# A four-layer graph network on one core: a 20-row tile in four column groups, its last ends moved into the next layer, and the last two output tiles in plain form

## The chip, the cores and the metric

The kernel runs on one core of one Trainium2 chip. The metric is the device time of one execution in microseconds (us); lower is better. A core has engines that run side by side, each in its own order: TensorE (PE, matrix products, with its weight loads listed apart as PEld), VectorE (DVE), ScalarE (ACT), GpSimd (POOL), and SyncE (SP), which here issues most DMAs. ACT and POOL issue DMAs too. Matmul results land in PSUM, which has eight banks per partition; everything else works on SBUF.

## The reference: what is computed

A graph with N = 2708 nodes, F = 256 features and a dense adjacency matrix `adj` (N x N, fp32) goes through four layers. After each layer the input is added and each row is normalised (mean 0, variance 1, eps 1e-5).

```python
# layer 0
x = layernorm(x + adj @ (x * w0))
# layer 1: graph attention, 4 heads of 64
e    = leaky_relu(src[:, :, None] + dst.T[None])      # masked by adj > 0, softmax over neighbours
x    = layernorm(x + layernorm(attn @ h) * gamma + beta)
# layer 2: three signed attention heads and two GRU cells
x    = layernorm(x + de * edge_output + dn * node_output)
# layer 3
deg  = adj.sum(1) + 1
h    = adj @ (x @ neigh_w.T) / deg
x    = layernorm(x + concat([x, h]) @ lin_w.T)
```

All arithmetic is fp32 unless noted.

## The kernel before, in words

Nodes are cut into NT = 22 tiles of 128 rows; 2708 is 21 x 128 + 20, so tile 21 has 20 rows. `adj_t` is the adjacency, padded to 22 x 128, cut into blocks of 128 x 128 that are transposed. Instructions are written in program order and a scheduler then fixes one order per engine; each engine works strictly through its own list, and semaphores tie the lists together.

**Layer 0** (L432 to L559). For each tile t a strip `adj_t[t]` (1408 KB) is loaded by SP, and `strip_matmul` (L201) adds up 22 products of 128 x 128 by 128 x 257 in one PSUM bank `acc`; the 257th column of the right side is 1 and yields the degree. An fp32 matmul shows as two PE instructions, so a tile is 44 instructions. Beside it `layer0_mask` and `layer0_own` read the strip on DVE and ACT. Then `layer0_rest(t - 1)` for the tile before: `layer0_scale` reads `acc`, `layernorm` (its `moments` use POOL for the power) and `layer1_projection`: two PE transposes (`tr`, L179), a copy by ACT, a projection (`pm`, L410), three exponentials by ACT, a product by DVE (`h`, L417), one more transpose (`pf`, L424), a copy and a DMA to `fall_d`. After the last strip, L558 and L559 run this for tiles 20 and 21, one after the other. Tile 21 uses 20 of the array's 128 columns but streams the same 257 columns per product.

**Layer 1** (L561 to L759). For each pair of column groups (`g` = 0, 2, 4: 1024, 1024 and 660 nodes) and each pair of heads `q`, a loop over the source tiles c = 0 to 21. Per c, DVE makes two weight tiles `p` (128 x 1024, L736) from a pool of six buffers, and PE multiplies them twice: `heads` (L718, results on 64 partitions, so two products side by side in the array) and `totals` (L727, results on 32 partitions, so four side by side). `step(c)`, once in each c, advances whatever generators are in the list `steps`: the ends of the group before. In g = 0 the list is empty. The last rows `h` of tiles 20 and 21 are first read at c = 20 and 21.

**Layer 2** (to L1232) ends with the generator `node`, whose pieces wait in the list `later`; `between()` runs one piece. PSUM is full there: `m1` takes one bank, `m26`, `m75`, `m43` two each, and all small work shares one bank called `bank`.

**Layer 3** (L1235 to L1283). The 2708 columns are cut in two halves of NH = 1354, the contraction in two halves as well, and each pair of chunks c (11 of them) is multiplied by a seven-product scheme (`seven`, L290) in place of eight. A half is cut in `units` of 512, 512 and 330 columns. Per unit and c, SP loads the block `p` (`load_pairs`, L240: one DMA for each run of whole tiles and contraction tile, one for each partial tile), DVE makes four sums, PE runs seven fp32 products (14 instructions) into the seven banks. At the end of a unit `gathered` (L313) combines the banks, and `rows3` (L1239) turns each tile back with two transposes, adds, normalises and stores it; its pieces run between the products of the next unit. In the first unit, `early3` chunks run beside what is left of `node`. For the third unit there is no next one: its rows run after the last product in a new set of banks (L1280 to L1283).

```python
L1279            later.append(rows3(u, y, o8))
L1280        ps_stack.close()
L1281        banks = ps_stack.enter_context(pool("ps_end", 8, space=PSUM))
L1282        while urgent or later:
L1283            between()
```

Of the kernel before, what the change touches and what calls it, by code (L numbers as in the profile page):

```python
# [19 lines left out]
P = 128  # L20
# [7 lines left out]
def kernel(  # L28
# [50 lines left out]
    MP = NT * P  # L79

    def sz(i):
        return min(P, N - i * P)
# [6 lines left out]

    def pieces(lo, w):  # L90

        while w:
            t, a = divmod(lo, P)
            b = min(P, a + w)
            yield t, a, b
            lo, w = lo + b - a, w - (b - a)

# [29 lines left out]
    x0 = [a[:, :F] for a in x0e]  # L127

    ends_at = [max(u for u, (a, w) in enumerate(units) for h in range(2) for p in pieces(h * NH + a, w) if p[0] == t) for t in range(NT)]
    by_end = sorted(range(NT), key=lambda t: ends_at[t])  # L130
# [108 lines left out]

    def load_pairs(units, u, c, s):  # L240

        a, w = units[u]
        for h in range(2):
            todo, at = list(pieces(h * NH + a, w)), 0
            while todo:

                t, lo, hi = todo.pop(0)
                n = 1
                while hi - lo == P and todo and todo[0][2] - todo[0][1] == P:
                    todo.pop(0)  # L250
                    n += 1
                m = n * (hi - lo)
                for i in range(2) if n > 1 else (slice(0, 2),):
                    src = adj_t[t : t + n, :, 2 * c + i, :].rearrange("t p n -> p t n") if n > 1 else adj_t[t, :, 2 * c : 2 * c + 2, lo:hi]
                    dst = s[:, i, h, at : at + m]
                    nc.sync.dma_start(dst.rearrange("p (t n) -> p t n", n=P) if n > 1 else dst, src)  # L256
                at += m
# [55 lines left out]
    def gathered(pool, m, w, wide, tag, bufs=1):  # L313

        m1, m26, m75, m43 = m
        m1s = pool.tile([P, wide], F32, tag="m1s", name="m1s", bufs=2)
        nc.scalar.copy(m1s[:, :w], m1[:, :w])
        y = pool.tile([P, FC, 2, wide], F32, tag=tag, name=tag, bufs=bufs)
        yq = y.rearrange("p f h w -> p (f h) w")[:, :, :w]
        nc.vector.tensor_tensor(  # L320
            yq[:, 0::3], m1s[:, None, :w].to_broadcast([P, 2, w]), m26[:, :, :w], ALU.add
        )
        nc.vector.tensor_tensor(
            yq[:, 1:3], yq[:, 3:4].to_broadcast([P, 2, w]), m75[:, :, :w], ALU.add
        )
        nc.vector.tensor_tensor(yq[:, 3], yq[:, 1], m75[:, 1, :w], ALU.add)
        return y, nc.vector.tensor_tensor(yq[:, 1:3], yq[:, 1:3], m43[:, :, :w], ALU.add)
# [57 lines left out]
    if True:  # L385
# [13 lines left out]
        if True:  # L399
# [5 lines left out]
            def layer1_projection(pool, t):  # L405
                n = sz(t)
                xt = transposed(ps_t, pool, xs[t], n, "xt")
                pm = ps_t.tile([P, 4, P], F32, tag="tr", name="pm").rearrange("p i q -> p (i q)")
                for f in range(FC):
                    nc.tensor.matmul(  # L410
                        pm[:n, : F + 2 * H], xt[:, f, :n], w1_a[:, f], start=(f == 0), stop=(f == FC - 1)
                    )
                nc.scalar.activation(rise[:n, t, :], pm[:n, F + H : F + 2 * H], AF.Exp, scale=1.0 - ALPHA)
                nc.scalar.activation(hs[t][:n, :, HD], pm[:n, F + H : F + 2 * H], AF.Exp, scale=ALPHA)
                fall = pool.tile([P, H], F32, tag="fall", name="fall", bufs=4)
                nc.scalar.activation(fall[:n], pm[:n, :H], AF.Exp, scale=ALPHA - 1.0)
                nc.vector.tensor_tensor(  # L417
                    hs[t][:n, :, :HD],
                    pm[:n, H : H + F].rearrange("p (h d) -> p h d", d=HD),
                    hs[t][:n, :, HD:].to_broadcast([n, H, HD]),  # L420
                    ALU.mult,
                )
                pf = ps_t.tile([P, 4, P], F32, tag="tr", name="pf")
                nc.tensor.transpose(pf[:H, 0, :n], fall[:n], ident[:n, :n])  # L424
                turned = pool.tile([H, P], F32, tag="turned", name="turned")
                nc.scalar.copy(turned[:, :n], pf[:H, 0, :n])
                nc.gpsimd.dma_start(fall_d[:, t * P : t * P + n], turned[:, :n])

                for g in [g for g, (lo, hi) in enumerate(spans[:4]) if hi == t + 1]:
                    load_fall(falls[g // 2], g, nc.gpsimd)  # L430

            with pool("l0", 2) as l0:  # L432
                w0_b = l0.tile([P, F], F32, name="w0_b", bufs=1)
                nc.scalar.dma_start(w0_b, bcast(w0, F))

# [26 lines left out]

                def layer0_rest(t, acc=None):
                    n = sz(t)
                    if acc is not None:
                        layer0_scale(t, acc)
                    nc.vector.tensor_tensor(xs[t][:n], xs[t][:n], x0[t][:n], ALU.add)
                    layernorm(xs[t], xs[t], n)
                    layer1_projection(l0, t)


                ahead = 3
                with pool("prep", side="right") as prep:
# [47 lines left out]
                    for t in range(ahead):  # L521
                        layer0_rest(t)
                    nw = weights(prep, "nw", neigh_w)
# [26 lines left out]
                nc.sync.dma_start(beta_b, bcast(beta, F))  # L550
                for t in range(ahead + 1, NT):
                    s = load_strip(l0, t)
                    last, acc = acc, ps_acc.tile([P, 512], F32, tag="acc", name="acc")
                    strip_matmul(acc[: sz(t), :FE], s, sz(t), lambda c: x0e[c])
                    layer0_mask(t, s)
                    layer0_own(t, s)

                    layer0_rest(t - 1, last)  # L558
                layer0_rest(NT - 1, acc)  # L559

            l1 = keep_stack.enter_context(pool("l1", 2))  # L561
            if True:

# [123 lines left out]
                for g in range(0, len(spans), 2):  # L687
# [6 lines left out]
                    cols = [(lo * P - at, width(lo, hi)) for lo, hi in segs]  # L694
                    sums, steps, halves = [], [], []

# [14 lines left out]
                    for q in range(H // 2):  # L711
# [20 lines left out]
                        for c in range(NT):  # L732
                            ps = []
                            for i in range(2):
                                p = l1.tile([P, 2 * W], F32, tag="p", name="p", bufs=6)
                                nc.vector.scalar_tensor_tensor(  # L736
# [264 lines left out]
    with (  # L1001
# [143 lines left out]

        def by_tiles(lo, w, src, ends):

            tiles, at = [], 0
            for t, c0, c1 in pieces(lo, w):
                got = src(at, c1 - c0)  # L1150
                at += c1 - c0
                if c1 - c0 < sz(t):
                    first = t not in ends
                    if first:
                        ends[t] = nleft.tile([P, FC, P], F32, tag=f"yt{t}", name=f"yt{t}")
                    nc.gpsimd.tensor_copy(ends[t][:, :, c0:c1], got)
# [78 lines left out]
        def complete(u):  # L1235

            return [t for t in by_end if ends_at[t] == u]

        def rows3(u, y, o8):  # L1239

            a, w = units[u]
            for h in range(2):
                for t, src in by_tiles(h * NH + a, w, lambda at, n: y[:, :, h, at : at + n], shared3):
                    n = sz(t)
                    o = o8[:, complete(u).index(t)]
                    pt = bank()
                    for f in range(FC):
                        nc.tensor.transpose(pt[:n, f * P : (f + 1) * P], src[:, f, :n], ident)
                    nc.vector.scalar_tensor_tensor(
                        o[:n], pt[:n, :F], rdeg[:n, t : t + 1], o[:n], ALU.mult, ALU.add  # L1250
                    )
                    mean, rs = moments(o, n)
                    nc.vector.scalar_tensor_tensor(mean, mean, -1.0, rs, ALU.mult, ALU.mult)
                    nc.scalar.activation(o[:n], o[:n], AF.Identity, scale=rs, bias=mean)
                    (nc.scalar if t % 2 else nc.sync).dma_start(out[t * P : t * P + n, :], o[:n])
                    yield


        lead = sorted(range(MH), key=lambda c: max(ends_at[2 * c], ends_at[2 * c + 1]))
        hq = {}  # L1260
        for u, (_, w) in enumerate(units):
            m = accumulators()
            for i, c in enumerate(lead):
# [6 lines left out]
                pa = nright.tile([P, 2, 2, W], F32, tag="p", name="p", bufs=3)  # L1270
                load_pairs(units, u, c, pa)
                if i == MH - 3:
# [6 lines left out]
            later.append(rows3(u, y, o8))  # L1279
        ps_stack.close()  # L1280
        banks = ps_stack.enter_context(pool("ps_end", 8, space=PSUM))  # L1281
        while urgent or later:  # L1282
            between()  # L1283
    hold_stack.close()
# [263 lines left out]
```

## Time and profile before

| what | value |
|---|---|
| median of three runs | 1902.06 us (1900.7, 1902.06, 1903.51) |
| the profiled execution, its own time | 1902.43 us |
| its span, first to last instruction | 1900.7 us |
| granted TensorE clock, mean of the span | 0.992 |
| PE busy | 1848.4 us (97%), 7475 instructions |
| DVE busy | 1283.9 us (68%) |
| ACT, POOL busy | 689.6 us (36%), 249.6 us (13%) |
| longest PE groups | L309 (seven products), L718 and L727 (layer 1), L203 (layer 0) |

In a page of the profile, a group of instructions is a line such as `L203 PE MATMUL acc<-turn,strip 128*128 128x257 f32 x836 | 191.6, 380 | 0.0`: source line, engine, operation, output and inputs by their names in the program, the weights' shape, the output's shape, the count; then busy time, mean duration of one in ns, and idle time of the engine just before. Matmuls are pipelined, so one lasts longer than the distance from its start to the next one's. That distance, the pitch, is what a stream of them costs; it is read from a timeline. In a timeline a line has start, length, engine, line, operation and count, and in brackets the idle time before it with what ended it. A table of windows gives the busy time of each engine in a stretch and, as PEclk, the share of full clock that TensorE was granted.

### The profile page before, as it was taken

Reading aid. Unit: us, or ns where it says so; the run is one execution under the profiler, and the core shown is the slowest. Engines: PE = TensorE matmul, PEld = TensorE weight load, DVE = VectorE, ACT = ScalarE, POOL = GpSimd, SP = SyncE. Lnnn points to the kernel's source line nnn. Section 1 sums busy time; section 2 is a strip of 40 time slices with the busy share of each in tenths; the row PEclk is TensorE's granted clock in tenths of the full one; section 3 lists DMA queues with packets and bytes.
Section 4 is the critical chain, followed back from the end, with each engine's and each line's share of the span. In section 5 each row is a group of like instructions: output and inputs, shape, how many; then the busy total and the mean of one; then the engine's idle time right before and its main releaser. Section 6 shows DMA issues by size and latency. Waiting matters only on the chain.

```text
span 1900.7 us, 22827 instructions
## 1 busy us (share of the span) xinstructions
PE 1848.4 (97%) x7475; PEld 1024.5 (54%) x7479; DVE 1283.9 (68%) x2279; ACT 689.6 (36%) x1418; POOL 249.6 (13%) x415
## 2 busy tenths in 40 slices
PE   8999989999999999999899999999999999999996
PEld 6888832223345887887344444444445555654444
DVE  4344469999797666554557888686877758855655
ACT  4444410033143204111455665555565555311101
POOL 1211210001012411000001001110200101211201
PEclk9999989999999999999999999999999999999998
DMA  8334400010002657554756666453554444733653
GB/s 293 130 145 152 167 23 1 1 29 7 17 1 55 150 130 208 129 126 111 209 141 187 184 166 177 115 159 97 165 150 119 121 113 129 191 111 98 194 155 107
DMA packets 432922, 235.89 MB, mean 124 GB/s; under 512 B 172150, under 2 KB 420620, under 8 KB 430364
## 3 DMA queue, kind: packets, MB, share of 16 engines
q1 hardware_dynamic: 416158, 207.40, 39.4%
q0 software_dynamic: 7760, 21.20, 3.4%
q10 hardware_dynamic: 8878, 5.76, 1.0%
q8 instruction: 61, 1.00, 0.2%
q14 instruction: 65, 0.53, 0.1%
HBM read 221.61 MB, written 12.65 MB: 123 GB/s over the span
## 4 chain that ended last, share of the span: by engine, by line
PE 85%; DVE 4%; DMA 4%; issue 2%; ACT 2%; POOL 1%; SPq 1%; ACTq 0%; DVEq 0%; POOLq 0%
PE m L309 39%; PE acc L718 11%; PE acc L203 8%; PE bank L1083 7%; PE den L727 6%; PE gate L958 4%; PE bank L1059 3%; PE bank L1134 2%; PE acc L510 1%; POOL bn_rs L167 1%; DMA strip<-in_adj_t_dram 1%; PE pm L410 1%; DVE p L1217 1%; SPq L256 1%; DMA blk<-in_adj_t_dram 1%
## 5 line engine op out<-in xcount | busy, mean ns | idle before, releaser
L736 DVE SCALAR_TENSOR_TENSOR p<-fall_b,rise,mask 128x1024 f32<-128x1024 f32 (+1 forms) x264 | 293.1, 1155 | 34.7 <-PE den L727 17.8
L1213 ACT ACTIVATE p<-st,e_neg 128x1024 f32<-128x1024 f32 (+1 forms) x198 | 197.2, 1040 | 206.6 <-PE m L309 202.6
L309 PE MATMUL m<-s,xq 128*128 128x512 f32 (+3 forms) x660 | 230.1, 467 | 0.0
L718 PE MATMUL acc<-p,h 128*64 128x512 f32 (+2 forms) x1056 | 216.6, 553 | 0.2 <-ACT sum L749 0.2
L203 PE MATMUL acc<-turn,strip 128*128 128x257 f32 (+1 forms) x836 | 191.6, 380 | 0.0
L309 PE MATMUL m<-p,xq 128*128 128x512 f32 (+1 forms) x396 | 183.1, 544 | 0.6 <-DVE p L297 0.3
L1216 ACT ACTIVATE p<-p 128x1024 f32<-128x1024 f32 (+1 forms) x198 | 178.9, 943 | 0.2
L309 PE MATMUL m<-p,x 128*128 128x512 f32 (+1 forms) x396 | 169.7, 547 | 5.1 <-DVE p L1217 4.8
L1217 DVE TENSOR_TENSOR p<-p,blk 128x1024 f32<-128x1024 f32 (+1 forms) x132 | 143.3, 1104 | 42.1 <-ACT p L1216 22.1
L203 PEld LDWEIGHTS acc<-turn,strip 128*128 128x128 f32 (+1 forms) x836 | 151.5, 185 | 25.3 <-issue 0.5
L309 PEld LDWEIGHTS m<-s,xq 128*128 128x128 f32 x660 | 124.3, 190 | 74.7 <-issue 58.2
L296 DVE TENSOR_TENSOR s<-p 128x512 f32<-128x512 f32 (+1 forms) x132 | 83.4, 633 | 119.6 <-PE m L309 104.3
L718 PEld LDWEIGHTS acc<-p,h 128*64 128x64 f32 x1056 | 70.5, 137 | 140.9 <-issue 131.7
L309 PE MATMUL m<-s,x 128*128 128x512 f32 (+3 forms) x330 | 127.4, 468 | 0.0
L727 PE MATMUL den<-p,h 128*32 128x512 f32 (+2 forms) x1056 | 118.2, 551 | 2.6 <-DVE p L736 2.6
L309 PEld LDWEIGHTS m<-p,x 128*128 128x128 f32 x396 | 74.8, 191 | 79.3 <-issue 60.9
L309 PEld LDWEIGHTS m<-p,xq 128*128 128x128 f32 x396 | 74.5, 190 | 78.1 <-issue 60.9
L452 ACT ACTIVATE below<-strip 128x384 bf16<-128x384 f32 x132 | 78.5, 594 | 70.9 <-DMA strip<-in_adj_t_dram 67.5
L1217 DVE TENSOR_TENSOR p<-p,turn 128x1024 f32<-128x1024 f32 (+1 forms) x66 | 72.0, 1112 | 20.3 <-ACT p L1216 12.2
L299 DVE TENSOR_TENSOR s<-p,s 128x512 f32<-128x512 f32 (+1 forms) x132 | 83.0, 629 | 2.0
L297 DVE TENSOR_TENSOR p<-p 128x512 f32<-128x512 f32 (+1 forms) x132 | 83.0, 629 | 1.7
L309 PEld LDWEIGHTS m<-s,x 128*128 128x128 f32 x330 | 61.7, 190 | 38.4 <-issue 34.1
(258 smaller groups left out, 2505.7 us busy)
## 6 DMA issues: line engine op xcount, KB each, us to landing
strip<-in_adj_t_dram SPq DMA_DIRECT2D x19, 1408.0 KB, 6.0
blk<-in_adj_t_dram SPq DMA_DIRECT2D x88, 256.0 KB, 3.3
blk<-in_adj_t_dram SPq DMA_DIRECT2D x88, 192.0 KB, 4.0
pa<-in_adj_t_dram SPq DMA_DIRECT2D x110, 128.0 KB, 2.6
turn<-in_adj_t_dram SPq DMA_DIRECT2D x44, 256.0 KB, 3.1
blk<-in_adj_t_dram SPq DMA_DIRECT2D x88, 128.0 KB, 2.4
p<-in_adj_t_dram SPq DMA_DIRECT2D x44, 256.0 KB, 3.4
turn<-in_adj_t_dram SPq DMA_DIRECT2D x44, 192.0 KB, 3.1
```

What stands on the lines that cost most here:

```text
L203: nc.tensor.matmul(acc, s[:, c, :n], rhs(c), start=(c == 0), stop=(c == NT - 1))
L296: nc.vector.tensor_tensor(s1, a21, a22, ALU.add)
L297: nc.vector.tensor_tensor(a21, a21, a11, ALU.subtract)
L299: nc.vector.tensor_tensor(s4, a12, s2, ALU.subtract)
L309: nc.tensor.matmul(dst[:, :w], lt, rt, start=start and not (one_bank and i), stop=stop and not (one_bank and i in (1, 2, 5)))
L718: nc.tensor.matmul(acc[s][i * HD : (i + 1) * HD, :ws], hs[c][:, 2 * q + i, :HD], ps[i][:, p0 : p0 + ws], **flags,)
L727: nc.tensor.matmul(den[j : j + CT, :ws], hs[c][:, 2 * q + i, HD + 1 - CT :], ps[i][:, p0 : p0 + ws], **flags,)
L736: nc.vector.scalar_tensor_tensor(p[:, :w], falls[g // 2][:, 2 * q + i, :w], rise[:, c, 2 * q + i : 2 * q + i + 1], mask[:, c, at : at + w] ...
L1083: nc.tensor.matmul(g[:, :w], lt, rt, start=(q == 0), stop=(q == len(terms) - 1))
L1213: nc.scalar.activation(p[:, :, :w], st_k[:, :, :w], AF.Relu, scale=-1.0, bias=e_neg[:, at, k : k + 1])
L1216: nc.scalar.activation(p[:, :, :w], p[:, :, :w], AF.Exp, scale=-1.0)
L1217: nc.vector.tensor_tensor(p[:, :, :w], p[:, :, :w], blk[:, i, :, :w], ALU.mult)
```

## The change

1. Layer 0's tile 21 (20 rows, at most CT = 32) is multiplied with 32-column weights; product c writes to partitions 32 (c mod 4) and up of `acc`, so that four of them are independent groups. ACT copies `acc` to `parts`, and one product with `quarter` (a 128 x 32 sum of identity columns) adds the four groups up (`layer0_last`).
2. `layer0_rest` and `layer1_projection` become generators. Those of tiles 20 and 21, with `layer0_last` between them, are put in `steps` of layer 1's g = 0, one piece for each c. `w0_b` and `quarter` move to a pool that lives on, and the helper tiles of these two ends to layer 1's pool. The scale of tile 20 stays in layer 0.
3. Layer 1's `p` has five buffers in place of six; `m1s` in `gathered` one in place of two.
4. Layer 3 leaves the last two full tiles (19 and 20) out of the seven-product scheme. The other 2452 columns make halves of NH3 = 1226, in units of 430, 430 and 366. `pieces` walks a list of tiles, and partial tiles fall at other places.
5. After the third unit, tiles 19 and 20 are multiplied in plain form (22 products of 128 x 128 by 128 x 256 each, the strip in two loads), into `m1` and `m26`; the rows of the third unit run between them, their transposes going round `bank`, `m75`, `m43`. There is no new set of banks.
6. `row3` holds back the last steps of a row (scale, ACT, store) until the next row's moments are issued (`flush`).

The diff, cut to its core:

```diff
+    last3 = [t for t in range(NT) if min(P, N - t * P) == P][-2:]
+    tiles3 = [t for t in range(NT) if t not in last3]
+    NH3 = (N - P * len(last3)) // 2
+    n3 = -(-NH3 // W)
+    w3 = min(W, (NH3 + P // 2) // n3)
+    units3 = [(a, min(w3, NH3 - a)) for a in range(0, NH3, w3)]
...
-        m1s = pool.tile([P, wide], F32, tag="m1s", name="m1s", bufs=2)
+        m1s = pool.tile([P, wide], F32, tag="m1s", name="m1s", bufs=1)
...
+            quarter = keep.tile([P, CT], F32, name="quarter")
+            nc.vector.tensor_reduce(quarter, ident.rearrange("p (j i) -> p i j", i=CT), AX.X, ALU.add)
...
+                def layer0_rest(pool, t):
                     n = sz(t)
                     nc.vector.tensor_tensor(xs[t][:n], xs[t][:n], x0[t][:n], ALU.add)
+                    mean, rs = moments(xs[t], n)
+                    yield
+                    nc.vector.tensor_scalar(xs[t][:n], xs[t][:n], mean, rs, ALU.subtract, ALU.mult)
+                    yield
+                    yield from layer1_projection(pool, t)
...
+                def layer0_last(t, parts):
+                    pq = ps_t.tile([P, 4, P], F32, tag="tr", name="pq").rearrange("p i q -> p (i q)")
+                    nc.tensor.matmul(pq[: sz(t), :FE], quarter[:, : sz(t)], parts[:, :FE], start=True, stop=True)
+                    layer0_scale(t, pq)
+                    yield
...
+                    for c in range(NT):
+                        j = c % TILES * CT
+                        nc.tensor.matmul(
+                            acc[j : j + CT, :FE], s[:, c, :CT], x0e[c], start=(c < TILES), stop=(c >= NT - TILES)
+                        )
...
+                layer0_scale(t - 1, last)
+                layer0_mask(t, s)
+                layer0_own(t, s)
+                    parts = keepr.tile([P, W], F32, tag="sum00", name="parts0")
+                    nc.scalar.copy(parts[:, :FE], acc[:, :FE])
...
+            rest = [layer0_rest(l1, NT - 2), layer0_rest(l1, NT - 1)]
+            if sz(NT - 1) <= CT:
+                rest.insert(1, layer0_last(NT - 1, parts))
...
-                    sums, steps, halves = [], [], []
+                    sums, steps, halves = [], [itertools.chain(*rest)] if g == 0 else [], []
...
-                                p = l1.tile([P, 2 * W], F32, tag="p", name="p", bufs=6)
+                                p = l1.tile([P, 2 * W], F32, tag="p", name="p", bufs=5)
...
+        ended = []
+        def flush():
+            while ended:
+                t, o, mean, rs = ended.pop()
+                n = sz(t)
+                nc.vector.scalar_tensor_tensor(mean, mean, -1.0, rs, ALU.mult, ALU.mult)
+                nc.scalar.activation(o[:n], o[:n], AF.Identity, scale=rs, bias=mean)
+                (nc.scalar if t % 2 else nc.sync).dma_start(out[t * P : t * P + n, :], o[:n])
+        def row3(t, o, acc):
+            n = sz(t)
+            nc.vector.scalar_tensor_tensor(o[:n], acc[:n, :F], rdeg[:n, t : t + 1], o[:n], ALU.mult, ALU.add)
+            mean, rs = moments(o, n)
+            flush()
+            ended.append((t, o, mean, rs))
...
-        for u, (_, w) in enumerate(units):
+        for u, (_, w) in enumerate(units3):
...
-                load_pairs(units, u, c, pa)
+                load_pairs(units3, u, c, pa, NH3, tiles3)
...
-        ps_stack.close()
-        banks = ps_stack.enter_context(pool("ps_end", 8, space=PSUM))
-        while urgent or later:
-            between()
+        free = itertools.cycle([None, "m75", "m43"])
+        per = -(-NT // 2)
+        for t, tag in zip(last3, ("m1", "m26")):
+            o = nleft.tile([P, F], F32, tag="y", name="y", bufs=3)
+            nc.gpsimd.dma_start(o, y3_d[t])
+            acc = ps_a.tile([P, W] if tag == "m1" else [P, 2, W], F32, tag=tag, name=tag)
+            acc = acc if tag == "m1" else acc[:, 0]
+            for lo in range(0, NT, per):
+                hi = min(lo + per, NT)
+                s = nright.tile([P, 2, 2, W], F32, tag="p", name="p", bufs=3).rearrange("p i h w -> p (i h w)")
+                s = s[:, : (hi - lo) * P].rearrange("p (c n) -> p c n", n=P)
+                nc.sync.dma_start(s, adj_t[t, :, lo:hi])
+                for c in range(lo, hi):
+                    nc.tensor.matmul(acc[:, :F], s[:, c - lo], h3[c], start=(c == 0), stop=(c == NT - 1))
+                    if c % 3 == 2 and (t != last3[0] or lo):
+                        between()
+            if t == last3[-1]:
+                while urgent or later:
+                    between()
+                flush()
+            row3(t, o, acc)
+        flush()
```

## The prediction

> **What bounds the kernel now.** I read the page's busy shares first, then a table of windows by stage, then the timeline of PE at the two places where PE is not full.
>
> ```profile
> PE 1848.4 (97%) x7475; PEld 1024.5 (54%) x7479; DVE 1283.9 (68%) x2279; ACT 689.6 (36%) x1418; POOL 249.6 (13%) x415
> ```
>
> PE is busy 97% of the span, so only two things can bring much: fewer columns through PE, or the few stretches where PE stands still. The windows name two such stretches, the passage from layer 0 to layer 1 and the end:
>
> ```profile
> 242.00:262.00 20.00, 15.43 (x67) 6.71 (x65) 8.07 (x20) 2.50 (x15) 4.92 (x8) 0.91 0.20 54
> 1882.00:1901.00 19.00, 2.63 (x17) 1.63 (x15) 10.01 (x39) 4.09 (x7) 4.27 (x9) 0.71 0.15 47
> ```
>
> Of the last 19.00 us PE works 2.63. The passage, PE alone (columns: start, length, engine, line, operation, count, idle time before):
>
> ```profile
> 245.33 8.44 PE L203 MATMUL acc<-turn,strip 128*20 128x257 f32 x38
> 253.70 0.44 PE L179 MATMUL tr<-ident,x 128*128 128x128 f32 x2
> 254.60 1.16 PE L410 MATMUL pm<-w_a,xt 128*128 128x264 f32 x4 [0.46 <-ACT xt L181]
> ...
> 257.88 1.38 PE L410 MATMUL pm<-w_a,xt 128*20 128x264 f32 x4 [0.34 <-ACT xt L181]
> ...
> 262.52 1.93 PE L727 MATMUL den<-p,h 128*32 128x512 f32 x8 [2.64 <-DVE p L736]
> 264.38 5.80 PE L718 MATMUL acc<-p,h 128*64 128x512 f32 x16
> 270.11 1.93 PE L727 MATMUL den<-p,h 128*32 128x512 f32 x16
> 271.96 3.65 PE L718 MATMUL acc<-p,h 128*64 128x512 f32 x16
> ```
>
> The 20-row tile costs as much as a full one (38 instructions in 8.37 us, start to start). Then the chains of tiles 20 and 21 run end to end, and PE waits for the first weights: 262.52 - 253.70 = 8.8 us from the end of the strip to layer 1. Note also the first two source tiles of layer 1: 7.59 us (262.52 to 270.11), where the next two take 5.44 (270.11 to 275.55). The third column from the end of a windows row is the granted clock, and tells why:
>
> ```profile
> 256.00:258.00 2.00, 0.69 (x4) 0.39 (x5) 0.88 (x3) 0.54 (x4) 1.49 (x3) 1.00 0.47 126
> 258.00:260.00 2.00, 1.45 (x5) 0.28 (x3) 0.34 (x1) 0.37 (x4) 0.35 (x1) 0.62 0.36 87
> 264.00:266.00 2.00, 2.00 (x8) 0.53 (x6) 2.00 (x3) 0.00 (x0) 0.00 (x0) 0.50 0.00 0
> ```
>
> The granted clock falls at about 259 us and is half at 264 to 266. The end, last product to last store:
>
> ```profile
> 1882.01 0.72 PE L309 MATMUL m<-s,turn 128*128 128x330 f32 x2
> ...
> 1892.30 0.44 DVE L1249 SCALAR_TENSOR_TENSOR o<-bank,rdeg,o 20x256 f32<-20x256 f32 x1
> ...
> 1895.16 0.59 ACT L1254 ACTIVATE o<-o,bn_mv,bn_rs 20x256 f32<-20x256 f32 x1
> 1895.78 0.55 ACTq L1255 DMA_DIRECT2D out_dram<-o  x1
> ```
>
> Seven rows go one after the other through DVE, POOL and ACT, with no product left to hide them.
>
> **The change, part by part.** All times are of the one profiled execution (1902.43 us, of which 1900.7 are span; the 1.7 outside stay). It lies 0.4 above the median of 1902.06, inside the runs' spread of 2.8, so the sum stands for both.
>
> *Tile 21 in four groups.* In layer 1, four `totals` products side by side have a pitch, per set of four, of 0.464 us at 512 columns (16 instructions in 1.855) and of 0.354 at 384 and 276 (16 in 1.415), while one full-width instruction of 512 columns takes 0.429 (24 in 10.3 us from 1754.85). So a set costs about its widest member plus 0.03. At 257 columns a full-width one takes 8.37 / 38 = 0.220 to 0.2285 (44 in 10.05 per tile); a set then costs 0.25, and 44 instructions are 11 sets, 2.8 in place of 10. For the 34 of them that come after the last insertion (`pf` of tile 19, 245.33), 2.1 us: the strip ends at 247.5. From both sides: nothing saved if the four don't overlap (34 x 0.22 = 7.5, 5.4 us later), or 0.354 a set if some fixed cost of the four weight loads binds (0.9 later). I take 0.25, because the row at 512 columns shows four at 1.08 times one. [...]
>
> *Tile 20's end stays in the passage.* In the changed kernel's instruction order PE still has `tr`, `pm`, `pf` of tile 20 ahead of layer 1, and behind them the one product `pq` that adds up the four groups. From `tr` to the end of `pf` took 2.6 us (253.70 to 256.3); ACT now copies `parts` ahead of `xt`, 257 columns, 0.4 by the rows of L749 at 276 columns (0.39), of which 0.3 shows; `pq` is two instructions, 0.46. Layer 1 can start at 247.5 + 2.6 + 0.3 + 0.5 = 250.9. Is DVE ready? Its order has eight `p` right after `h` of tile 19, which ended at 246.05. The first `p` needs only `fall_b`; the second may wait for the strip's buffer (247.5), so two are done by 249 and the third by 250.1. Yes. 250.9 against 262.52: **-11.6**.
>
> *The clock.* 7.59 - 5.44 = 2.15 us were lost to half clock. [...] the longest gap here is 2.64 and the clock had fallen before it began, with PE at 3.43 of 6 us busy (254 to 260). [...] a half-busy stretch is enough. Judged by the trace, the changed passage (1.7 us of work in 3.4, from 247.5 to 250.9) is half-busy too, but short[...]. [...] **-2.15**; by the trace's worst, 0. I take the gain.
>
> *Tile 21's end in layer 1.* Its PE work moves into a full stretch: two `tr` (0.12), four `pm` (0.92), one `pf` (0.1), and the pieces wait for nobody's data long, being a c or more apart: **+1.25**. DVE gets ten small operations (about 3 us). It needs 2.4 of the 2.72 us per c, so it regains that in ten c, and it starts with a lead of two or three `p`; the 20 c until `h` of tile 20 is read cover ACT's and POOL's part. POOL's `fall_d` store of tile 21 is read only for g = 4, 250 us later.
>
> *Five buffers.* With PE working on two `p`, three are ahead in place of four. I followed DVE's and PE's instruction order with the trace's durations (DVE 1.20 per `p` of 1024 columns, 0.82 of 660, 0.40 per 256-column operation; PE 1.79 + 0.93 per c): no stall with five or six. With DVE 6% slower five lose 0.5. **+0.2**, between 0 and 1.
>
> *Layer 3, columns.* Pitch of an instruction: 0.4293 at 512, 0.2768 at 330, so 0.3606 at 430 and 0.3070 at 366 on a straight line. 154 instructions per unit: 154 x (2 x 0.4293 + 0.2768) = 174.9 before, 154 x (2 x 0.3606 + 0.3070) = 158.3 after, -16.6. Plain tiles: 2 x 44 x 0.2285 = +20.1. PE ends its products with all rows' transposes done but the last: 0.22 a tile, five more than at 1882, +1.1. Waits: before, those over 0.15 us add up to about 5 until 1882; one of 1.12 ahead of 1854.54, a transpose behind a DVE that stood waiting for POOL's power, goes with `flush`. Shorter products (-0.14 per pair) hide less of `node`'s bank changes; the instruction order already puts two products where one stood, so +1. Sum: PE's last product comes **+4.6** later, passage and clock aside.
>
> *Layer 3, queues.* SP issues seven loads per c now in unit 2, eight after in units 1 and 2. 32 loads took 16.37 us from 1857.84, 0.51 each, so eight take 4.1, against a c of 14 x 0.307 = 4.3 (5.05 in units 0 and 1). It fits, with little over in unit 2; three stores also stand in SP's list there, 0.4 each. The strips of the plain tiles take the buffers of chunks 9 to 11 and of the first half strip: 720 KB each, every 5.0 us, where a 1408 KB strip lands in 6.0. Costed at nothing; if late, each 1 us is 1 us. POOL's two loads of `y3_d` are issued a unit's length ahead.
>
> *Layer 3, end.* Before: 1882.57 (last product's end) to 1900.7, 18.1 us. After, one row is left: 0.35 to DVE, sum and moments 0.95, POOL 0.2 + 0.55, DVE and ACT 0.8, all from the rows of the last tile above, then 4.9 from issue to the end (1895.78 to 1900.7): 7.8. **-10.3**. The eight rows of unit 2 have eleven slots of 1.37 us, and DVE needs 1.33 for one; they begin 5 us after the unit's end, when `gathered` (2.4 us then, plus POOL's copies) is done.
>
> `m1s` and `w0_b` cost nothing: its copies are tens of us apart. Layer 2's orders are unchanged.
>
> Sum: -11.6 - 2.15 + 1.25 + 0.2 + 4.6 - 10.3 = -18.0: **1884.5 us**.
>
> **The rivals.** (1) The clock falls again. The stretch's half load speaks for it, its brevity against: +2.15, and a late `p` 1 more: 1887 to 1888. (2) Layer 3 gives nothing: strips or blocks late at the changes of unit (as at 1836.90, 0.56 us behind a load), or `node`'s waits grow by 0.14 at each of 37 bank changes (5 us), which together eat the 5.7: 1890. Against it: SP's 0.51 and the order. (3) Slower than before: small pieces. New pieces are 8, 36, 38 and 46 columns wide, 32 to 184 bytes a packet. In units 0 and 1 (1766 to 1834 us) 25846 packets took 60.2% of 16 engines, 25 ns each. Unit 1 has 2304 packets per c, 3.6 us in 5.05. Were they dearer, all 33 chunks would run at the DMAs' pace. At 34 ns it begins, at 40 the whole gain is gone, at 45 it is 1915. Against: in unit 2 now 8048 of 18291 packets are under 512 B and q1's took 53.4%, 23 ns each. (4) The four groups don't overlap: 1890.
>
> **How the numbers follow.** The sum as it stands 0.52, (1) 0.20, (2) 0.18, (4) 0.04, (3) 0.04, of which half ends slower, and 0.02 for several losses at once, half of them slower too. Low end 1881: the sum less 3.5 (waits of layer 3 gone as well). High end 1893: (1) and (2) together. A difference of 0.2% (3.8 us) is about what measurements of this kernel tell from none. Faster by more 0.94, within 0.03, slower 0.03.
>
> **What would show it.** PE's first `den` near 251 with the first two c in 5.5 us and the clock at 1.00 (right), or 0.50 in 252 to 257 (1). The 32-column products: sets of four in 0.25. Layer 1's PE never waiting for a `p` after its first. The plain products without a DMA wait, the last one some 8 us before the end. In the chunks of 366 columns PE waiting for DMA, chunk after chunk, would be (3). Wrong altogether if the passage still ends after 258, or the end is over 12 us.

## The result, and the profile after

| | before | after |
|---|---|---|
| median | 1901.38 us (4 runs, 1900.04 to 1903.51) | 1885.57 us (4 runs, 1883.11 to 1887.16) |
| profiled execution, its span | 1902.43, 1900.7 us | 1887.16, 1885.1 us |
| ratio of the times | | 0.9915, 95% interval 0.9898 to 0.9932 |

The change brings 15.8 us, where the prediction's sum was 18.0; the time of 1885.57 us lies in the predicted range of 1881 to 1893, near its 1884.5. Not every term of the sum held. PE's row of the page:

```profile
PE 1843.0 (98%) x7565; PEld 1037.4 (55%) x7565; DVE 1278.9 (68%) x2280; ACT 690.1 (37%) x1419; POOL 254.2 (13%) x419
```

PE is 5.4 us less busy in a span that is 15.6 shorter, so some 10 us were standing time. The windows of the two stretches (columns: stretch, length, PE, PEld, DVE, ACT and POOL busy, granted clock, DMA share, GB/s):

```profile
242.00:262.00 20.00, 19.10 (x134) 6.70 (x134) 18.18 (x23) 2.24 (x11) 3.83 (x5) 1.00 0.15 40
258.00:260.00 2.00, 2.00 (x14) 0.57 (x14) 2.00 (x5) 0.00 (x0) 0.00 (x0) 1.00 0.01 4
264.00:266.00 2.00, 2.00 (x16) 0.49 (x16) 2.00 (x4) 0.00 (x0) 0.00 (x0) 1.00 0.30 86
1874.00:1885.00 11.00, 0.37 (x2) 0.00 (x0) 2.75 (x11) 1.80 (x3) 1.58 (x3) 0.63 0.15 44
```

In the passage PE is busy for 19.10 of 20 us (15.43 before), and the clock is full. The end without products is 11 us in place of 18. PE's timeline of the passage (in layer 1, `den` is what `totals` writes and `acc` what `heads` writes):

```profile
244.46 2.35 PE L589 MATMUL acc<-turn,strip 128*32 128x257 f32 x34
246.74 0.44 PE L187 MATMUL tr<-ident,x 128*128 128x128 f32 x2
247.69 1.16 PE L419 MATMUL pm<-w_a,xt 128*128 128x264 f32 x4 [0.51 <-ACT xt L189]
249.24 0.27 PE L434 MATMUL pf<-ident,fall 128*4 128x128 f32 x1 [0.40 <-ACT fall L425]
249.44 0.39 PE L491 MATMUL pq<-parts,quarter 128*20 128x257 f32 x1
249.45 0.64 PE L772 MATMUL den<-p,h 128*32 128x512 f32 x3
...
250.84 3.65 PE L763 MATMUL acc<-p,h 128*64 128x512 f32 x16
254.42 1.92 PE L772 MATMUL den<-p,h 128*32 128x512 f32 x16
```

The last 34 instructions of the 20-row tile take 2.28 us start to start: 8.5 sets of four, 0.268 each. Before, the last 38 took 8.37, which is 7.5 for 34. Layer 1's first `den` starts at 249.45 (262.52 before), and the two `pq` stand between the first `den`, not ahead of them. Further milestones, before and after: layer 1's second stretch of `den` 270.11 and 254.42; its last stretch of `den` 606.62 and 592.14; layer 3's first product 1650.48 and 1636.43; the last product's end 1882.73 and 1874.37; the span's end 1900.7 and 1885.1. So the passage and layer 1's first stretch brought 15.7 us, the end of tile 21 took 1.2 back within layer 1, layer 2 lost 0.4, layer 3 delayed PE by 5.7 and shortened the end by 7.2. The end, in the timeline of all engines:

```profile
1869.89 4.48 PE L1358 MATMUL m<-turn,p 128*128 128x256 f32 x20
...
1872.37 0.16 DVE L1291 SCALAR_TENSOR_TENSOR bn_mv<-bn_mv,bn_rs 128x1 f32<-128x1 f32 x1 [0.72 <-POOL bn_rs L175]
1872.46 0.48 DVE L1298 SCALAR_TENSOR_TENSOR o<-bank,rdeg,o 128x256 f32<-128x256 f32 x1
...
1873.66 0.15 DVE L174 TENSOR_SCALAR bn_rs<-bn_mv 128x1 f32<-128x1 f32 x1
1873.96 0.54 POOL L175 TENSOR_TENSOR bn_rs<-bn_rs,neg_half 128x1 f32<-128x1 f32 x1 [1.62 <-DVE bn_rs L174]
1874.53 0.16 DVE L1291 SCALAR_TENSOR_TENSOR bn_mv<-bn_mv,bn_rs 128x1 f32<-128x1 f32 x1 [0.72 <-POOL bn_rs L175]
1874.62 0.47 DVE L1298 SCALAR_TENSOR_TENSOR o<-m,rdeg,o 20x256 f32<-20x256 f32 x1
...
1876.71 0.47 DVE L1298 SCALAR_TENSOR_TENSOR y<-m,rdeg,y 128x256 f32<-128x256 f32 x1
...
1879.59 0.33 SPq L1293 DMA_DIRECT2D out_dram<-y  x1
```

A row takes DVE 2.16 us (1872.46 to 1874.62), of which 0.72 are a wait for POOL: L1291, the step that `flush` was to hold back, stands on DVE behind the moments of its own row and ahead of the next row. DVE's waits between 1860 and 1880 (awaited instruction: us in total, times, longest):

```profile
DVE bn_mv L1291 <- POOL bn_rs L175: 6.3, 9, 0.7
```

The last row (tile 20, `y`) starts at 1876.71, 2.3 us after its products ended.

### The profile page after: what moved, and what is told of

Same layout as the page of the kernel before. It is cut to its first block, busy times and chain, and to the rows that moved or that the text cites. A ratio compares the mean times of both kernels' runs of the same rounds, so it can differ in the third digit from the quotient of the medians.

```text
span 1885.1 us, 23118 instructions
## 1 busy us (share of the span) xinstructions
PE 1843.0 (98%) x7565; PEld 1037.4 (55%) x7565; DVE 1278.9 (68%) x2280; ACT 690.1 (37%) x1419; POOL 254.2 (13%) x419
## 5 line engine op out<-in xcount | busy, mean ns | idle before, releaser
L211 PE MATMUL acc<-turn,strip 128*128 128x257 f32 x792 | 181.5, 379 | 0.0
L304 DVE TENSOR_TENSOR s<-p 128x512 f32<-128x512 f32 (+3 forms) x132 | 81.6, 619 | 121.5 <-PE m L317 104.7
L211 PEld LDWEIGHTS acc<-turn,strip 128*128 128x128 f32 x792 | 147.3, 190 | 20.3
L1128 PE MATMUL bank<-xt,whh 128*128 128x512 f32 (+3 forms) x192 | 81.7, 548 | 1.4 <-DMA xt<-xt 1.2
L305 DVE TENSOR_TENSOR p<-p 128x512 f32<-128x512 f32 (+3 forms) x132 | 81.6, 618 | 1.9
```

Source lines behind the costliest of these rows:

```text
L211: nc.tensor.matmul(acc, s[:, c, :n], rhs(c), start=(c == 0), stop=(c == NT - 1))
L304: nc.vector.tensor_tensor(s1, a21, a22, ALU.add)
L305: nc.vector.tensor_tensor(a21, a21, a11, ALU.subtract)
L1128: nc.tensor.matmul(g[:, :w], lt, rt, start=(q == 0), stop=(q == len(terms) - 1))
```

## The experiments

All times are medians; each ratio is to the kernel before on the same chip (1901.39 us for runs 1 to 4, 1901.90 for 5 to 8, 1902.79 for 9 and 10). Where a run is set against the changed kernel, that is its 1885.57 from a set with 1901.38, so such a difference can be off by about 1 us: by the ratios, run 8's 7.6 would be 6.5. My theory after the result: layer 0 gave nearly all, by three things that can be told apart (groups, moved end, clock); layer 3 gave 1.5, because short products beside layer 2's closing steps and DVE's waits for POOL ate its gain. The rival was the prediction's split: 12.3 and 5.7.

**1. Layer 0's part alone.** The changed kernel with `complete` to the end of layer 3 as before (one line of the cut stands for all):

```diff
...
-        for u, (_, w) in enumerate(units3):
+        for u, (_, w) in enumerate(units):
...
```

> The changed kernel with layer 3 as it was before: the four column groups, the moved end of tile 21 and the five weight buffers alone. My theory, from the two traces: the passage gave 13.1 us at layer 1's first product and 15.7 at its third source tile, of which layers 1 and 2 gave back some 1.6, so it should be 14.0 to 14.5 us below the kernel before (about 1887.2), and layer 3 gave only 1.5. Rival, the prediction's own split: layer 0 and its clock 12.3 (1889.1), layer 3 5.7.

Measured 1887.19 us, ratio 0.9922 (0.9908 to 0.9935): 14.2 us below before. The theory holds; the prediction's 12.3 lies just outside the interval, which is 12.4 to 17.5.

**2. Layer 3's part alone.** The kernel before with the changed layer 3 (shown against the kernel before, again one line for all):

```diff
...
-        for u, (_, w) in enumerate(units):
+        for u, (_, w) in enumerate(units3):
...
```

> The kernel before with the changed kernel's layer 3 (three even units, plain tiles, rows held back) and nothing else. My theory: 1.5 us below the kernel before, between 0.5 and 2.5, since PE's last product comes 5.8 us later by itself and the end behind it is 7.3 us shorter. Rival, the prediction's split: 5.7 us below (4.6 later, 10.3 shorter).

Measured 1900.56 us, ratio 0.9993 (0.9984 to 1.0001): 0.8 us, between 3.0 and nothing. 5.7 is excluded. Layer 3's first product to its last one's end took 238.2 us here, 237.9 in the changed kernel, 232.2 before. The two parts add up: 14.2 + 0.8 = 15.0 against 15.8.

**3. POOL makes the product of a row.**

```diff
-                nc.vector.scalar_tensor_tensor(mean, mean, -1.0, rs, ALU.mult, ALU.mult)
+                nc.gpsimd.tensor_tensor(mean, mean, rs, ALU.mult)
...
             mean, rs = moments(o, n)
+            nc.vector.tensor_scalar(mean, mean, -1.0, None, ALU.mult)
```

> The changed kernel, but the product of mean and 1/deviation that closes a row of layer 3 is made on POOL, behind POOL's own power, so that DVE waits for POOL in no row (DVE only negates the mean). My theory: DVE's 2.16 us a row fall to about 1.4, the row of tile 20 starts when its products have ended instead of 2.4 us behind them, and the end behind the last product falls from 10.8 to between 8.5 and 9.5 us: 1.3 to 2.3 us below the changed kernel. Rival: the end hangs on PE's last product, ACT and the store alone, DVE's rows being hidden: no change, or up to 0.4 slower by POOL's second operation in the last row.

Measured 1885.21 us, ratio 0.9914 (0.9901 to 0.9928): no change from the changed kernel. Yet the rows did what the theory said. Its timeline has the last row right behind the last product's end (1872.41):

```profile
1872.45 0.48 DVE L1298 SCALAR_TENSOR_TENSOR y<-m,rdeg,y 128x256 f32<-128x256 f32 x1 [2.89 <-PE m L1359]
...
1875.49 0.33 SPq L1293 DMA_DIRECT2D out_dram<-y  x1
```

Rows are 1.51 us apart, and the last store is issued 3.1 us after the last product, not 5.2. But from there to the span's end (1883.4) it takes 7.9 us, where the changed kernel takes 5.5. The sequencers' records of the closing lines show where (line, sequencer, operation, count, shortest/median/longest ns, first and last start). In the changed kernel POOL goes from its branch to the next step in 0.5 us:

```profile
L1584 POOLq COMPARE_BRANCH  x1: 50/50/50, 1878.7 to 1878.7; - x1
...
L1584 POOLq EVENT_SEMAPHORE  x1: 17/17/17, 1879.2 to 1879.2; - x1
```

and here in 2.9, and only then begins POOL's drain of 4.39 us (4392 ns, the longest of three):

```profile
L1585 POOLq COMPARE_BRANCH  x1: 50/50/50, 1875.2 to 1875.2; - x1
...
L1585 POOLq EVENT_SEMAPHORE  x1: 17/17/17, 1878.1 to 1878.1; - x1
```

```profile
L1628 POOLq DRAIN  x3: 50/106/4392, 1878.2 to 1883.2; - x3
```

1878.2 + 4.39 = 1882.6, the span ends 0.8 later. What the rows gave, POOL's way out took. DVE and ACT stand as long behind their branches (3.2 and 3.3 us in the changed kernel). POOL has 22 instructions more here than in the changed kernel, one for each row tile; in run 5, where it has 22 fewer, it stands 2.5 us behind its branch as well (1855.6 to 1858.1). What it waits for there is not shown.

**4. Units of 512, 384 and 330.**

```diff
-    units3 = [(a, min(w3, NH3 - a)) for a in range(0, NH3, w3)]
+    units3 = [(0, W), (W, 3 * P), (W + 3 * P, NH3 - W - 3 * P)]
```

> The changed kernel with layer 3's units cut at 512, 896 and 1226 columns (512, 384, 330 wide) in place of 430, 430, 366: the products that stand between the closing steps of layer 2 are 512 columns long again, and a source tile has 6, 6 and 7 loads. The columns are the same in sum. My theory, that the waits beside the closing steps come from products too short to cover a change of bank: PE's excess waits there fall from 7.6 us towards the 3.1 of the kernel before, 3 to 4 us below the changed kernel. Rival, that they come from the order in which the steps stand: no change within 1 us.

Measured 1879.65 us, ratio 0.9881 (0.9866 to 0.9896): 5.9 us below the changed kernel. PE's waits beside layer 2's closing steps (engine, line, awaited instruction: us in total, times, longest), first in the kernel before:

```profile
PE m L309 <- DMA p<-in_adj_t_dram: 0.5, 1, 0.5
```

then in the changed kernel:

```profile
PE m L317 <- DMA p<-in_adj_t_dram: 0.5, 1, 0.5
PE bank L1170 <- DVE y L1181: 0.4, 1, 0.4
PE bank L1179 <- DVE y L1160: 0.4, 1, 0.4
PE bank L1157 <- POOL yt L1201: 0.3, 1, 0.3
PE bank L1128 <- ACT g_r L1133: 0.2, 1, 0.2
PE bank L1157 <- DVE yt L1217: 0.2, 1, 0.2
```

and with the aligned units:

```profile
PE m L317 <- DMA p<-in_adj_t_dram: 0.2, 1, 0.2
```

Five waits for the closing steps' own data, 1.5 us in sum, are gone. They are only the idle time that the profile shows. Counting each instruction at its pitch (0.361 us at 430 columns, 0.429 at 512, 0.278 at 330, 0.109 for a transpose) finds more: beside the closing steps 7.3 of 103.3 us are waiting in the changed kernel, 3.2 of 104.3 before, and 3.2 of 104.3 here. A pair of products of 512 columns covers what a pair of 430 does not. Run 4 has fewer loads for each c too, but in either kernel PE waits for a load only once there (0.5 and 0.2 us), so the loads do not explain it. PE's stay in layer 3 falls from 237.9 to 234.3 us, the 3 to 4 expected. Another 2.0 are at the end, which is 8.7 us long behind the last product in place of 10.7; here the rows have run up to it (tile 20's starts at 1869.49, its products ended at 1869.08). This version beats both kernels.

**5. The rows without POOL.**

```diff
+        if own:
+            nc.vector.reciprocal(rstd[:n], rstd[:n])
+            nc.vector.tensor_scalar(mv[:n, 0:1], mv[:n, 0:1], -1.0, None, ALU.mult)
+            return mv[:n, 0:1], rstd[:n]
...
-                nc.vector.scalar_tensor_tensor(mean, mean, -1.0, rs, ALU.mult, ALU.mult)
+                nc.scalar.activation(rs, rs, AF.Sqrt)
+                nc.scalar.activation(mean, mean, AF.Identity, scale=rs)
...
-            mean, rs = moments(o, n)
+            mean, rs = moments(o, n, own=True)
```

> The changed kernel, but layer 3's rows close without POOL: DVE takes the reciprocal and negates the mean, ACT takes the square root and the product. My theory, from the sequencers' records of the runs so far: the end does not hang on the last store but on POOL, whose closing drain of 4.39 us starts only behind its last power (1879.3 in the changed kernel, 1878.2 with POOL's product, 1895.2 before) and ends 1.0 to 1.4 us before the span does. With POOL free since about 1862 the end is set by the last row and by ACT's and DVE's 3 us behind their closing branch: 10.8 us behind the last product become 7 to 8.5, so 2.3 to 3.8 us below the changed kernel. Rival, the prediction's reading: the end comes 5 to 5.5 us behind the issue of the last store, whatever POOL does; the rows are no shorter, so no change within 1 us.

Measured 1883.84 us, ratio 0.9908 (0.9893 to 0.9923): 1.7 below the changed kernel, less than the 2.3 to 3.8 expected and with intervals that overlap. In the trace the end shrank as expected, from 10.7 to 8.1 us (1873.34 to 1881.4). Its last row:

```profile
1873.38 0.48 DVE L1303 SCALAR_TENSOR_TENSOR y<-m,rdeg,y 128x256 f32<-128x256 f32 x1 [2.83 <-PE m L1363]
...
1876.15 0.33 SPq L1298 DMA_DIRECT2D out_dram<-y  x1
```

But the theory behind it fell: the last store is issued 2.8 us behind the last product, and the span ends 5.2 after that, as the prediction's reading has it (4.9 before, 5.5 in the changed kernel), although POOL's drain began at 1858.2. So POOL's drain (4.39 us) is one of several parts of the way out, beside DVE's and ACT's stand behind their branches (3.1 and 2.7 us here); it is the last one only in run 3, where it began 2.7 us behind the last store's issue (0.3 ahead of it in the changed kernel, 0.6 before). What was won is the rows' delay.

**6. Both.** Runs 4 and 5 in one kernel.

> The units cut at 512 and 896 columns and, in the same kernel, the rows closed without POOL. The two gains lie in different stretches (products beside layer 2's closing steps; behind the last product), so they should add: 1879.7 less 2 to 3.5, about 1877. Rival: the rows already ran up to the last product with the aligned units (tail 8.7 us), so the second change brings under 1 us here.

Measured 1879.58 us, ratio 0.9880 (0.9865 to 0.9896): nothing on top of run 4, where about 1877 was expected. The rival holds: the end is 8.2 us in place of 8.7, and with the rows at the last product there was no more to win.

**7. Both ends ahead of layer 1.**

```diff
                 rest.insert(1, layer0_last(NT - 1, parts))
+            finish(itertools.chain(*rest))
...
-                    sums, steps, halves = [], [itertools.chain(*rest)] if g == 0 else [], []
+                    sums, steps, halves = [], [], []
```

> The changed kernel with the last tile in four column groups, but with the ends of tiles 20 and 21 run to their end ahead of layer 1 in place of between its steps. It tells what the clock hangs on. Theory, that a stretch of some 8 us at about half load lets the granted clock fall, as in the kernel before: layer 1's first den about 6 us later than in the changed kernel, 1.25 us back from layer 1, and the clock at 0.5 in the first source tiles (+2.15): about 7 us above the changed kernel, 1892.5. Rival, that it needed the full-width strip ahead of it or was chance: the clock stays at 1.00, about 5 above, 1890.5.

Measured 1889.07 us, ratio 0.9933 (0.9920 to 0.9947), 3.5 above the changed kernel. It does not answer its question: the scheduler kept the end of tile 21 on PE between layer 1's first products all the same (`tr` of tile 21 at 258.66, first `den` at 249.77). The granted clock stayed at 1.00; layer 1 took 1.6 us longer, 0.57 of it one wait for a `p`. Both expectations rested on an order that did not come about.

**8. Tile 21 in full width, its end moved.**

```diff
-                if sz(t) <= CT:
+                if False:
                     for c in range(NT):
...
```

> The changed kernel with tile 21's products in full width, one behind the other, its end still moved into layer 1. 34 instructions of 0.220 us stand in the passage in place of sets of four of 0.268 (2.3 us), the first ten cost 1.5 us more, and the sum of the four groups and its copy (0.8) are gone. Theory: 5.5 to 6.5 us above the changed kernel, about 1891.5, with the clock at 1.00. Rival, that the groups' gain is taken back by what stands behind them (DVE's first weights late): under 3 us above.

Measured 1893.18 us, ratio 0.9949 (0.9936 to 0.9963): 7.6 above the changed kernel by the medians, a little over the 5.5 to 6.5 expected; in the trace 6.9 at the first `den` and 7.0 in the span. The groups are worth about 7, the moved end the other 6 of the 13.1 us by which the first `den` came earlier (262.52 to 249.45):

```profile
244.97 8.44 PE L211 MATMUL acc<-turn,strip 128*20 128x257 f32 x38
253.34 0.44 PE L187 MATMUL tr<-ident,x 128*128 128x128 f32 x2
...
256.37 1.06 PE L772 MATMUL den<-p,h 128*32 128x512 f32 x8 [0.26 <-DVE p L781]
257.37 3.65 PE L763 MATMUL acc<-p,h 128*64 128x512 f32 x16
```

The clock stays at 1.00 in this trace with PE busy for 3.06 of 4 us (254 to 258) behind the same long strip. So moving the end was enough to keep the clock, without the groups.

**9. The kernel before, kept busy.**

```diff
+                for _ in range({NT - 2: 1, NT - 1: 2}.get(t, 0)):
+                    idle = ps_t.tile([P, 4, P], F32, tag="tr", name="idle").rearrange("p i q -> p (i q)")
+                    for f in range(FC):
+                        nc.tensor.matmul(
+                            idle[:n, : F + 2 * H], xt[:, f, :n], w1_a[:, f], start=(f == 0), stop=(f == FC - 1)
+                        )
```

> The kernel before, with products whose results nobody reads in the holes of its passage: one set of four behind the last transpose of tile 20's end, two behind that of tile 21's, so that PE works about 1.8 of every 2 us between 254 and 262. They read what has just been read and stand on nobody's way, at worst 0.3 us ahead of a transpose. Theory, that a long half-busy stretch lowers the clock: it stays at 1.00, the first two source tiles of layer 1 take 5.44 us in place of 7.59, and the kernel is about 2 us faster than before, 1899.4. Rival, that the clock falls for something else (the layers' change, DVE's load): no gain, or 0.5 slower by the products.

Measured 1899.91 us, ratio 0.9985 (0.9978 to 0.9991): 2.9 us faster, 1.7 to 4.2, by products that nobody reads. Timeline and windows:

```profile
262.48 1.96 PE L428 MATMUL idle<-w_a,xt 128*20 128x264 f32 x8
265.20 1.06 PE L733 MATMUL den<-p,h 128*32 128x512 f32 x8 [0.77 <-DVE p L742]
266.20 3.65 PE L724 MATMUL acc<-p,h 128*64 128x512 f32 x16
269.78 1.92 PE L733 MATMUL den<-p,h 128*32 128x512 f32 x16
```

```profile
260.00:262.00 2.00, 1.59 (x8) 0.51 (x6) 0.13 (x1) 0.19 (x1) 1.23 (x2) 1.00 0.30 72
266.00:268.00 2.00, 2.00 (x14) 0.66 (x12) 2.00 (x3) 0.00 (x0) 0.00 (x0) 1.00 0.01 4
```

The first 8 `den` and 16 `acc` take 4.58 us at full clock (265.20 to 269.78); before they took 7.59. So the clock cost 3.0 us in the profiled execution of the kernel before, and filling the passage was enough to keep it. It went with PE's load there: PE is busy for 4.73 us of 256 to 262 in this trace, and for 3.98 in run 10's, whose passage is that of the kernel before and starts within 0.2 us of this one; there the clock is 0.50 from 262 to 268.

**10. Five buffers alone.**

```diff
-                                p = l1.tile([P, 2 * W], F32, tag="p", name="p", bufs=6)
+                                p = l1.tile([P, 2 * W], F32, tag="p", name="p", bufs=5)
```

> The kernel before with five buffers for layer 1's weights in place of six, nothing else. Theory: 0 to 0.2 us slower, within the measurement, since PE waits for no weight behind the first in the changed kernel's trace. Rival: five are too few where DVE's lead is short, at the start of layer 1 and at its changes of group: 2 us or more slower.

Measured 1902.03 us beside 1902.79, ratio 0.9995 (0.9987 to 1.0003): no cost that can be measured, and no wait for a `p` behind the first.

## Why the prediction was right, and where not

- *The four groups and the passage* (-11.6): right in its mechanism, -13.1. A set of four at 257 columns took 0.268 us, near the 0.25 taken from the row at 512 columns, 3.3 times one instruction's 0.220. From `tr` to the first `den` 2.71 us, not 3.4: the copy of `parts` delayed nothing and `pq` came behind the first `den`.
- *The clock* (-2.15, rival 1): right in sign, mis-sized. That so short a passage keeps the clock was my estimate; it stayed at 1.00 in every 2 us window from 240 to 272. The step took 5.44 us as the full-clock price of the first stretch, but that is the pitch of 32 instructions, and the first stretch has 24. Run 9 shows 4.58 for them, so the loss was 3.0. It is not the same in every execution: run 2, whose passage is that of the kernel before, took 6.14 us (262.30 to 268.44) and run 10 took 6.12, a loss of 1.6 and 1.5. The fall did not wait for a long gap: in the kernel before the clock fell at about 259 us, and the longest gap in the passage until then was 0.83 us. From its timeline, then from run 2's:

```profile
257.25 0.29 PE L179 MATMUL tr<-ident,x 20*128 20x20 f32 x2 [0.83 <-DVE x L173]
```

```profile
262.30 1.94 PE L735 MATMUL den<-p,h 128*32 128x512 f32 x8 [2.65 <-DVE p L744]
264.17 4.34 PE L726 MATMUL acc<-p,h 128*64 128x512 f32 x16
268.44 1.92 PE L735 MATMUL den<-p,h 128*32 128x512 f32 x16
```

Where the passage is unchanged the clock fell: to 0.50 in the kernel before and in run 10, and in run 2 by its 6.14 us. Where it is moved or filled it stayed at 1.00, in the changed kernel and in runs 7, 8 and 9.
- *Tile 21's end in layer 1* (+1.25): right, +1.2 (15.69 earlier at the second stretch of `den`, 14.48 at the last).
- *Five buffers* (+0.2): nothing measurable (run 10).
- *Layer 3, columns* (-16.6 + 20.1): the plain products' pitch is 0.216 us in the stream of 24 from 1853.45 (5.18 us), not 0.2285, so +19.0 for 88; the others are as estimated (0.361 and 0.308), so -16.3.
- *Layer 3, waits* (+1): the step that was mis-sized. It counted on the two products that stand where one stood; 430 columns were too short all the same. Beside the closing steps 7.3 us are waiting against 3.2 before: +4.1, near the 5 of rival 2, and run 4 takes it away. In the later chunks waits fell by 2.2, 1.1 of which the step had expected. With 1.1 for the transposes PE ended 5.7 later, not 4.6 (-16.3 + 19.0 + 1.1 + 4.1 - 2.2).
- *Layer 3, end* (-10.3): the step that failed, -7.2. "DVE needs 1.33 for one" row left out the wait for POOL that it had itself priced, on the ground that `flush` removes it. The order of instructions, which could be read beforehand, has L1291 ahead of the next row's L1298: what program order puts off, the scheduler put back. Rows need 2.16 us where slots are about 1.5, so they end behind the last product. The end was costed at 7.8 us and took 10.7: 2.3 are the late start of the last row, 0.6 the way out (5.5 from the last store to the end, not 4.9). In runs 3 and 5, where DVE doesn't wait for POOL, the last store is issued 3.1 and 2.8 us behind the last product, not 5.2. (In the kernel before, the last product ends at 1882.73, its start plus its length, 0.16 later than the prediction has it.)
- *Small pieces* (rival 3) and groups that do not overlap (rival 4) fell: PE waits for no DMA between 1738 us and its last product, the strips of the plain tiles included, and four groups in 0.268 us do overlap, which run 8 prices.

Layer 0, costed at 12.3, brings 14.2 by run 1 and 14.0 in the traces; layer 3, costed at 5.7, brings 0.8 by run 2 and 1.5 in the traces. So the forecast was 2 us too low in one place and 4 to 5 too high in another, and in the sum these partly cancel: 18.0 for 15.8. That is luck. So is part of the nearness of 1884.5 to 1885.57: the sum starts from the profiled execution's 1902.43, and the four runs of the kernel before have their median at 1901.38.

## What to carry to other kernels

The hole in PE's work cost twice here, as 8.8 us between the strip and layer 1, with PE busy for 3.43 of 6 of them, and as 3.0 us lost to the lowered clock behind it (run 9): move work out of such a hole into a full stretch before shortening the work, and price the stretch behind it by counting its instructions. Products beside another chain's bank changes were too short at 430 columns (7.3 us of waiting) and not at 512 (3.2); widths that are equal in sum were not equal there, so put the widest where they cover. A step held back in program order must be looked for in the scheduled order, or given to an engine on which nobody waits.

One hole of this kind is left in the changed kernel, as it was before (4.76 us ahead of 912.98, the clock 0.50 from 912 to 916): at the first products of a later layer PE waits for DVE, and the clock falls.

```profile
897.79 1.22 PE L317 MATMUL m<-p,x 128*128 128x512 f32 x1 [4.76 <-DVE p L1262]
```

```profile
896.00:900.00 4.00, 2.21 (x3) 1.12 (x4) 4.00 (x5) 0.29 (x1) 0.00 (x0) 0.64 1.03 375
```

No run here fills it.

## What the runs showed of the hardware

The way out of the program took 4.9 to 5.5 us from the issue of the last store (7.9 in run 3), and its parts overlap: in the kernel before, the changed one and runs 3, 5 and 6 there was a drain of 4.39 us on POOL, and in the kernel before, the changed one and runs 5 and 6 DVE and ACT stood 2.5 to 3.3 us behind their closing branches. Where POOL's drain began 0.6 and 0.3 us ahead of the last store's issue (before and after) or 18 us ahead (run 5), the way out took 4.9, 5.5 and 5.2 us; where it began 2.7 behind (run 3), 7.9. Small tiles in column groups were nearly as good at 257 columns as at 512: a set of four took 0.268 us where one full-width instruction takes 0.220, and 0.464 where one takes 0.429, so 3.3 and 3.7 times the rate.
